# Four elementwise operations of a softplus go from VectorE to GpSimd in eight parts, in a software-pipelined scan stage

## The chip, the cores and the metric

The kernel runs on one core of a Trainium2 chip. The metric is device time in microseconds, the median of several executions; lower is better. The engines are named as the profile names them: PE is the matmul engine (PEld its weight loads), DVE is VectorE, ACT is ScalarE, POOL is GpSimd, and SP is the queue that issues most DMAs. Each engine works through its own instructions in the order in which they were written; semaphores tie the engines together.

## The reference

The program is two layers of a graph network with a mixture of experts behind each. Only the middle of the first layer matters here, a selective scan (Mamba) over 4096 tokens with 512 channels and 16 states per channel:

```python
u = silu(xconv)
dbc = u @ w_xp
dt = softplus(dbc[:, :DT_RANK] @ w_dt + b_dt)
dA = exp(dt[:, :, None] * A[None])
dBu = dt[:, :, None] * B[:, None, :] * u[:, :, None]
# scan over the tokens: h = dA*h + dBu ; y = h @ C
y = (ys + u * D_skip) * silu(z)
```

The change touches the softplus and the product dt·u. Everything else (the adjacency product before, the experts and the second layer behind) is the same program in both kernels.

## The kernel before, in words

**Tiling.** Tokens go through in 8 chunks of 512 (`CW`), numbered 0 to 7. The 512 channels are 4 blocks of 128 partitions, `m` = 0 to 3; blocks 0 and 1 are the first pair ("half 0"), 2 and 3 the second. Each chunk has 32 steps (`STEPS`); a step takes one channel block and two of the 16 states. Steps 0 to 15 of a chunk work on the first pair, steps 16 to 31 on the second.

**One step** (`Step`), for step n, is spread over four engines:

- POOL multiplies `du` (= dt·u, one block, used for both states) with the broadcast row of B into `db`, 128x1024 (L1354). The multiply of step n+1 is issued during step n. `db` has two buffers, so it must wait until step n-1 has read the same buffer.
- ACT makes the decays `da` = exp(dt·A), one 128x512 tile in PSUM per state (L1370), one step ahead, in three PSUM banks.
- DVE runs two scans in place over `db` (L1377), with `da` from PSUM, and then the product `hc` = `db`·`cb` (L1387). A small ACT copy saves the last column as state (L1383).
- POOL's queue issues a DMA that adds the second half of `hc` to the first (L1391, `pair`), one step late; PE then sums `hc` over the states with an identity matmul (L1404), up to three steps late.

B and C rows come in by broadcast DMAs on SP (L1350), double-buffered.

**The next chunk's front.** While chunk c is scanned, everything that chunk c+1 needs is made in between, at step numbers written out by hand in `Front.PLAN` and `Front.EARLY` (L899 to L914): "EARLY" pieces come between a step's scans and its product, the others after it. At step 26 ACT takes exp(-|x|) into `du`, at step 27 ("plus", L1071) `t1` = 1 + that, at step 28 ("log", L1075) the logarithm into `du`. Each is one 128x1024 instruction per pair of blocks. At steps 28 to 31 DVE runs `do_soft`, four operations, each once per pair, so eight 128x1024 instructions per chunk:

- soft 0 (L1081): `t1` = (`t1` - 1) - e, the rounding error of 1 + e with its sign turned, where e is the exponential,
- soft 1 (L1085): `du` = log - `t1`,
- soft 2 (L1087): `dt` = max(x, 0) + `du`, which is the softplus,
- soft 3 (L1089): `du` = `dt`·u.

At step 31 the EARLY piece comes ahead of the step's other work, since the multiply for the next chunk's step 0 needs `du` of the first pair. The second pair's `dt` and `du` are first used by work issued in step 15 of the next chunk. Chunk 0's front runs before the scan stage.

**Order.** In this stage PE, DVE, ACT and POOL keep the written order. In each step the loop at L1501 writes: the next step's inputs (L1524, B and C loads and the POOL multiply), the `pair` DMA of the step before (L1526), the scans with the next step's decays, the EARLY piece, the product, the gates of finished sums (L1413, a DVE multiply of a PSUM tile with `zs`), and the rest of the front. Adjacency matmuls for chunk c+2 (L871) fill PE.

**Buffers the change uses.** `t1` shares a slot (tag "tmp") with `xc`, which the next front takes at step 13. The pool tag "h" holds the normalised rows from step 9 until step 13 of a chunk.

Of the kernel before, what the change touches and what calls it, by code (L numbers as in the profile page):

```python
# [10 lines left out]
F32 = mybir.dt.float32  # L11
BF16 = mybir.dt.bfloat16
I32 = mybir.dt.int32
AF = mybir.ActivationFunctionType
ALU = mybir.AluOpType
# [4 lines left out]
P = 128  # L20
CW = 512
# [25 lines left out]
def kernel(ctx: ExitStack, tc: tile.TileContext, out: bass.AP, **a):  # L47
    nc = tc.nc
    x, adj, adjT = a["x"], a["adj"], a["adjT"]
# [28 lines left out]
    def load(pool, src, name, eng=None):  # L78
        t = pool.tile(list(src.shape), F32, name=name)
        (eng or nc.sync).dma_start(t, src)  # L80
        return t

    def load_bcast(pool, vec, name):
        t = pool.tile([P, vec.shape[1]], F32, name=name)
        nc.sync.dma_start(t, vec.to_broadcast([P, vec.shape[1]]))
        return t
# [696 lines left out]
    with ExitStack() as s1:  # L783
        wp = s1.enter_context(tc.tile_pool(name="w_gnn0", bufs=1))
        w1p = s1.enter_context(tc.tile_pool(name="work1", bufs=1))
# [53 lines left out]
        H = MB // 2  # L839
        GS = NS // 2  # L840
        STEPS = H * 2 * GS
# [9 lines left out]
        psts, fronts = {}, {}  # L851
# [41 lines left out]
        class Front:  # L893
# [175 lines left out]
            def do_plus(self):  # L1069
                for a in range(2):  # L1070
                    nc.scalar.activation(self.t1[:, a], self.du[a], AF.Identity, bias=1.0)  # L1071

            def do_log(self):
                for a in range(2):
                    nc.scalar.activation(self.du[a], self.du[a], AF.Ln, bias=1.0)  # L1075

            def do_soft(self, i):
                for a in range(2):
                    t1, dt, du = self.t1[:, a], self.dt[a], self.du[a]
                    if i == 0:  # L1080
                        nc.vector.scalar_tensor_tensor(  # L1081
                            t1, t1, -1.0, du, ALU.add, ALU.subtract
                        )
                    elif i == 1:
                        nc.vector.tensor_tensor(du, du, t1, ALU.subtract)  # L1085
                    elif i == 2:
                        nc.vector.tensor_tensor(dt, dt, du, ALU.add)  # L1087
                    else:
                        nc.vector.tensor_tensor(  # L1089
                            du, dt, self.us[:, a * H:a * H + H, :], ALU.mult  # L1090
                        )
                if i == 3:
                    fronts[self.c] = self

        def keep_gated(c):

            yd = dram.tile([P, MB, CW], F32, name=f"yd{c}")
            nc.sync.dma_start(yd, fronts[c].us)
            return yd
# [130 lines left out]


        SLOW = 3

        TAILS = {(NC - 2, i): 0 for i in (25, 26, 28)}
        TAILS.update({(NC - 2, i): 2 for i in range(29, STEPS)})
# [179 lines left out]
        with tc.manual_schedule(engines={  # L1415
# [13 lines left out]
            for _ in range(2 * NT + 2 - sum(FILLED.values())):  # L1429
                i = min(range(STEPS), key=lambda i: pe[i] - PE_RATIO * dve[i])  # L1430
# [4 lines left out]
            def advance(k=1, wait=False):  # L1435


                while k > 0:
                    k -= 1
                    if next(prop, None) and wait:  # L1440
                        break
                return k
# [19 lines left out]

            gate_w = load(const, a["L0_ffn_gate_w"], "gate_w")
            gate_b = load_bcast(const, a["L0_ffn_gate_b"], "gate_b")
            carry = wp.tile([P, MB, KC - 1], F32, name="carry")
            state = wp.tile([P, MB, NS], F32, name="state")

# [10 lines left out]
            fr = Front(0)  # L1478
# [22 lines left out]
            for n in range(NC * STEPS):  # L1501
                c, i = divmod(n, STEPS)
                if n == 0:
                    cur = Step(0, 0)
                    cur.inputs(None)
                    das = [cur.decay(0), cur.decay(1)]
                steps.append(cur)
                if i == 5 and c > 0:
                    if c < NC - 1:
                        kept[c - 1] = keep_gated(c - 1)  # L1510
                    else:
                        tails.extend(Tail(c - 1, hh) for hh in range(2))
                if i == 8 and c == NC - 2:
                    tails.extend(
                        Tail(k, hh, kept[k], k < SLOW) for k in range(c) for hh in range(2)
                    )
                if i == 8:
                    fr = Front(c + 1) if c + 1 < NC else None
                    prop = propagation(c + 2) if c + 2 < NC else iter(())
                if i == STEPS - 1 and fr is not None:  # L1520
                    fr.at(i, Front.EARLY)
                nxt = Step(*divmod(n + 1, STEPS)) if n + 1 < NC * STEPS else None
                if nxt is not None:
                    nxt.inputs(cur)  # L1524
                if n > 0:
                    steps[n - 1].pair()  # L1526
                old, das = das, []
                for j in range(2):
                    cur.scan(j, old[j])
                    if nxt is not None:  # L1530
                        das.append(nxt.decay(j))
                if 7 < i < STEPS - 1 and fr is not None:
                    fr.at(i, Front.EARLY)
                if c == NC - 1 and i in NORMS:
                    NORMS[i]()
                cur.product()
                for k in gated:
                    steps[k].gate()
                gated = []
                while summed < n - 1 and (summed < n - 3 or not steps[summed].paired):  # L1540
                    steps[summed].total()
                    gated.append(summed)
                    summed += 1
                if i < 8:
                    fronts[c].at(STEPS + i)
                elif fr is not None:
                    fr.at(i)
                for _ in range(TAILS.get((c, i), 1)):
                    Tail.step(tails)
                if c == NC - 1:  # L1550
                    for piece in NPIECES.get(i, ()):
                        piece()
                    if i == 22:
                        last = Last()
                        last.first(1)
                    elif i == 24:
                        last.fetch()
                    elif i == 25:
                        last.first(0)
                    elif i in (27, 28):  # L1560
                        last.residual(i - 27)
                owed = advance(pieces[i] + owed, True)
                if i == 7:
                    while owed:
                        owed = advance(owed, True)
                cur = nxt
            n = NC * STEPS
# [17 lines left out]
    wp = ctx.enter_context(tc.tile_pool(name="w_ffn0", bufs=1, reuse_waits="tile"))  # L1585
    early.close()
    with ExitStack() as s2:
# [309 lines left out]
        with tc.manual_schedule(engines={  # L1897
# [10 lines left out]
            for k, (c, j2) in enumerate(seq):  # L1908
# [11 lines left out]
                if k in ROUTES:  # L1920
                    b = ROUTES[k]
# [47 lines left out]
    with ExitStack() as s4:  # L1969
# [21 lines left out]
        ready, op = list(range(SPLIT)), []  # L1991
# [31 lines left out]
    with tc.If(again > 0):  # L2023
        with ExitStack() as s3:
# [3 lines left out]
            with tc.For_i(0, NT, 1) as i:  # L2028
                f = gp.tile([P, N], F32, name="f_all")
# [51 lines left out]
        with ExitStack() as s3:  # L2081
# [20 lines left out]
            op = s3.enter_context(tc.tile_pool(name="out2", bufs=1))  # L2102
# [71 lines left out]
```

## Time and profile before

| what | value |
|---|---|
| median of 6 runs | 2361.13 us (2353.97 to 2365.89) |
| the profiled execution | 2355.22 us |
| its span, first to last instruction | 2353.3 us |
| scan stage in the span | about 158 to 1244 us |
| one chunk in the steady part | 136.0 us (step 31's POOL multiply at 563.19, 699.20 and 835.21 us) |
| DVE, POOL, ACT, PE busy in 440 to 580 us (140 us) | 136.16, 107.52, 83.84, 135.52 us |
| TensorE clock granted in that stretch | 0.98 |

A timeline line gives the start in us from the span's start, the duration in us, the engine, the line of the kernel, the operation, the tiles and shapes, and in square brackets how long the engine was idle before it and what ended the wait. "x2" merges two neighbours of the same kind. A line of stretches gives, for PE, PEld, DVE, ACT and POOL, the busy time and the number of instructions, then the granted clock, the DMA share and GB/s. DVE instructions follow each other somewhat more closely than their durations say: an `hc` of 1.23 us is followed 1.14 us after its start.

### The profile page before, as it was taken

How to read it: one execution, taken by the hardware profiler on the slowest of the kernel's cores; microseconds unless marked ns; L12 is line 12 of the kernel's file. 1: busy time of each engine (PE TensorE's matmuls, PEld its weight loads, DVE VectorE, ACT ScalarE, POOL GpSimd, SP SyncE). 2: the span in 40 equal slices, each digit the busy share in tenths (PEclk: the TensorE clock that was granted, in tenths of full speed). 3: DMA queues.
4: the chain of work that ended last, by engine and by line, in shares of the span. 5: the costliest groups of instructions: out<-in, count | busy, mean ns of one | idle time of the engine just before them, and what ended most of it. 6: DMA issues, size and time to landing. Idle time of an engine off the chain costs nothing. (4 is left out here: it accounts for less than half of the span.)

```text
span 2353.3 us, 28092 instructions
## 1 busy us (share of the span) xinstructions
PE 2105.1 (89%) x8235; PEld 1498.8 (64%) x8235; DVE 1812.8 (77%) x3207; ACT 1193.4 (51%) x2064; POOL 1399.7 (59%) x1056
## 2 busy tenths in 40 slices
PE   7899999999999999997896899968869899799894
PEld 6665564656556565654564787855648678577773
DVE  6959999999999999999997887125228899854242
ACT  4145657565665755567672223214459578433221
POOL 1037778777777777786763444531357778745651
PEclk9999999999999999998897999988969999899997
DMA  8559999999999999998985999743345555476794
GB/s 285 172 156 258 234 271 242 272 245 250 271 238 272 244 273 244 250 268 237 280 260 168 312 335 321 232 157 109 128 123 176 165 165 171 122 229 213 232 317 153
DMA packets 302677, 532.29 MB, mean 226 GB/s; under 512 B 31323, under 2 KB 170575, under 8 KB 301616
## 3 DMA queue, kind: packets, MB, share of 16 engines
q1 hardware_dynamic: 244720, 416.84, 54.8%
q0 software_dynamic: 57792, 113.54, 21.8%
q8 instruction: 69, 1.13, 0.2%
q14 instruction: 96, 0.79, 0.1%
HBM read 434.34 MB, written 49.02 MB: 205 GB/s over the span
## 5 line engine op out<-in xcount | busy, mean ns | idle before, releaser
L1354 POOL TENSOR_TENSOR db<-du,bb 128x1024 f32<-128x1024 f32 x256 | 607.1, 2372 | 312.5 <-DVE hc L1387 75.6
L1377 DVE TENSOR_TENSOR_SCAN db<-da,state,db 128x512 f32<-128x512 f32 x512 | 627.4, 1267 | 20.2 <-ACT da L1370 18.0
L871 PE MATMUL pt<-at,gn 128*128 128x256 f32 x2048 | 481.6, 388 | 17.5 <-ACT gn L129 10.4
L871 PEld LDWEIGHTS pt<-at,gn 128*128 128x128 f32 x2048 | 398.7, 195 | 139.3 <-issue 62.7
L1370 ACT ACTIVATE da<-dt,negA 128x512 f32<-128x512 f32 x512 | 346.1, 688 | 245.7 <-DVE db L1377 235.9
L1387 DVE TENSOR_TENSOR hc<-db,cb 128x1024 f32<-128x1024 f32 x256 | 327.6, 1280 | 17.9 <-issue 0.4
L1864 PE MATMUL pf<-gn,f 128*128 128x256 f32 x1280 | 300.3, 393 | 27.5 <-issue 27.4
L1864 PEld LDWEIGHTS pf<-gn,f 128*128 128x128 f32 x1280 | 250.5, 197 | 71.9 <-issue 36.8
L1404 PE MATMUL psy<-hc,ident 128*128 128x512 f32 x560 | 291.6, 614 | 1.9 <-DMA hc<-hc 1.9
L712 PE MATMUL ps_h<-xkT,wk 128*128 128x256 f32 x864 | 215.5, 391 | 16.5 <-ACT hk L716 6.7
L697 PE MATMUL ps_y<-wk,hk 128*128 128x256 f32 x864 | 216.4, 385 | 3.9 <-issue 3.7
L702 DVE TENSOR_TENSOR yk<-ps_y,bk 128x512 f32<-128x512 f32 x73 | 50.4, 690 | 214.4 <-PE ps_y L697 146.9
L1391 POOL DMA_DIRECT2D hc<-hc x232 | 201.9, 870 | 0.2
L712 PEld LDWEIGHTS ps_h<-xkT,wk 128*128 128x128 f32 x864 | 159.2, 193 | 55.5 <-ACT hk L716 15.4
L1726 POOL DMA_INDIRECT x<-gnd,ls_idx x128 | 153.1, 1196 | 68.0 <-issue 22.6
L697 PEld LDWEIGHTS ps_y<-wk,hk 128*128 128x128 f32 x864 | 162.5, 193 | 27.1 <-issue 4.9
L1404 PEld LDWEIGHTS psy<-hc,ident 128*128 128x128 f32 x560 | 105.1, 194 | 82.4 <-issue 60.1
L1726 POOL DMA_INDIRECT ring<-gnd,ls_idx x88 | 110.5, 1255 | 53.5 <-DVE x L1742 31.7
L1846 ACT ACTIVATE f<-at 128x1024 f32<-128x1024 f32 x80 | 84.2, 1053 | 91.3 <-remote 51.1
L999 PE MATMUL ps_xz<-hT,w_in 128*128 128x512 f32 x256 | 117.0, 600 | 14.1 <-ACT hT L983 7.5
L716 ACT ACTIVATE hk<-ps_h,d0r_b 128x256 f32<-128x256 f32 x104 | 48.8, 472 | 136.2 <-PE ps_h L712 77.8
L1016 PE MATMUL ps_xz<-xc,dK 128*128 128x512 f32 x256 | 114.8, 592 | 0.0
(398 smaller groups left out, 2999.6 us busy)
## 6 DMA issues: line engine op xcount, KB each, us to landing
at<-in_adjT_dram SPq DMA_DIRECT2D x208, 512.0 KB
bb<-bcd SPq DMA_DIRECT2D x128, 512.0 KB
cb<-bcd SPq DMA_DIRECT2D x128, 512.0 KB
hc<-hc POOLq DMA_DIRECT2D x232, 256.0 KB
wk<-in_L_ffn_W_dram SPq DMA_DIRECT2D x70, 512.0 KB
wk<-in_L_ffn_expert_w_dram SPq DMA_DIRECT2D x114, 256.0 KB
ls_at<-in_adj_dram SPq DMA_DIRECT2D x32, 512.0 KB
hc<-in_adj_dram SPq DMA_DIRECT2D x16, 512.0 KB
```

Source lines behind the costliest of these rows:

```text
L697: nc.tensor.matmul(ps[:, j, :], hT[:, m, j * P:(j + 1) * P], w[:, m, :], start=(m == 0), stop=(m == kb_out - 1),)
L712: nc.tensor.matmul(ps[:, j, :], w[:, d, m * P:(m + 1) * P], xT[:, d, :], start=(d == 0), stop=(d == DB - 1),)
L871: nc.tensor.matmul(pt[:, k, :], xl[:, j, k * P:(k + 1) * P], at[:, jj, :], start=(j == 0 and k == 0), stop=(j == NT - 1 and k == DB - 1),)
L999: nc.tensor.matmul(ps, w_in[:, k, m * P:(m + 1) * P], self.hT[:, k, :], start=(k == 0), stop=(k == DB - 1),)
L1354: nc.gpsimd.tensor_tensor(self.db, self.f.du[self.half][:, self.mi:self.mi + 1, :].to_broadcast([P, 2, CW]), self.bb, ALU.mult,)
L1370: nc.scalar.activation(da, self.f.dt[self.half][:, self.mi, :], AF.Exp, scale=negA[:, self.m, n:n + 1])
L1377: nc.vector.tensor_tensor_scan(self.db[:, j, :], da, self.db[:, j, :], state[:, self.m, n:n + 1], ALU.mult, ALU.add,)
L1387: nc.vector.tensor_tensor(self.hc, self.db, self.cb, ALU.mult)
L1391: nc.gpsimd.dma_start(self.hc[:, 0, :], self.hc[:, 1, :], accum_op=ALU.add)
L1404: nc.tensor.matmul(f.psy[m], ident, self.hc[:, j, :], start=False, stop=(self.g == GS - 1 and j == last),)
L1726: nc.gpsimd.indirect_dma_start(out=to[:, :], out_offset=None, in_=gnd[:, :], in_offset=bass.IndirectOffsetOnAxis(ap=lists.idx[:, q, s:s + ...
L1864: nc.tensor.matmul(pf[:, t, :], f[:, jj, t * P:(t + 1) * P], gn[:, j, :], start=(j == 0 and t % 2 == 0), stop=(j == NT - 1 and t % 2 == 1),)
```

## The change

For chunks 1 to 7, DVE keeps `do_soft` for the first pair only. The second pair's four operations go to POOL, each cut into its two channel blocks: eight `tensor_tensor` instructions of 128x512. They are written into the loop right behind the `pair` DMA, so in POOL's order they come after the multiply for the next step and ahead of the one after it, in steps 29, 30 and 31 of the chunk in which the front is made and in steps 1, 2, 4, 6 and 8 of the next.

GpSimd gets plain two-input operations only. Soft 0 has three terms, so ACT subtracts 1 from the second pair's `t1` in an extra 128x1024 instruction at step 27 (with a constant tile `minus1` as its bias). The logarithm of the second pair is written to its own tile `ln1`, in the slot with tag "h", because e in `du` is still needed by a POOL operation that comes later. Chunk 0 is as before.

```diff
             def do_plus(self):
                 for a in range(2):
                     nc.scalar.activation(self.t1[:, a], self.du[a], AF.Identity, bias=1.0)
+                if self.c > 0:
+                    nc.scalar.activation(
+                        self.t1[:, 1], self.t1[:, 1], AF.Identity, bias=minus1[:, :1]
+                    )
 
             def do_log(self):
+                to = list(self.du)
+                if self.c > 0:
+                    to[1] = self.ln1 = w1p.tile([P, H, CW], F32, name="ln1", tag="h")
                 for a in range(2):
-                    nc.scalar.activation(self.du[a], self.du[a], AF.Ln, bias=1.0)
+                    nc.scalar.activation(to[a], self.du[a], AF.Ln, bias=1.0)
+
+            def spare(self, n):
+                i, b = divmod(n, H)
+                t1, dt, du = self.t1[:, 1, b, :], self.dt[1][:, b, :], self.du[1][:, b, :]
+                out, x, y, op = (
+                    (t1, t1, du, ALU.subtract), (du, self.ln1[:, b, :], t1, ALU.subtract),
+                    (dt, dt, du, ALU.add), (du, dt, self.us[:, H + b, :], ALU.mult),
+                )[i]
+                nc.gpsimd.tensor_tensor(out, x, y, op)
 
             def do_soft(self, i):
-                for a in range(2):
+                for a in range(2 if self.c == 0 else 1):
...
+        SPARES = {29: 0, 30: 1, 31: 2, 1: 3, 2: 4, 4: 5, 6: 6, 8: 7}
...
+            minus1 = wp.tile([P, 1], F32, name="minus1")
+            nc.gpsimd.memset(minus1, -1.0)
...
                 if n > 0:
                     steps[n - 1].pair()
+                if i in SPARES:
+                    f = fronts[c] if i < STEPS // 2 else fr
+                    if f is not None and f.c > 0:
+                        f.spare(SPARES[i])
```

The eight POOL parts are called spare 0 to spare 7 below, by the number that `SPARES` gives them.

## Prediction

> **What bounds the kernel now.** I read the page's busy shares first, then a table of stretches, the waits of DVE in the scan stage, and the timelines of DVE, POOL and ACT around a chunk's boundary.
>
> ```profile
> 440.00:580.00 140.00, 135.52 (x446) 83.83 (x445) 136.16 (x124) 83.84 (x147) 107.52 (x68) 0.98 0.97 257
> ...
> DVE db L1377 <- ACT da L1370: 18.0, 21, 2.4
> DVE db L1377 <- POOL db L1354: 2.2, 1, 2.2
> DVE hc L1387 <- issue: 0.4, 1, 0.4
> ```
>
> DVE is busy 136.16 of 140 us and in the whole stage (160 to 1240 us) waits 20.6 us on others, so an instruction taken off DVE looks worth its time. PE is busy 135.52 us: a gain above some 4.5 us per chunk would run into PE. POOL, at 107.52 us, looks free. A regular step shows that it isn't free in a useful place:
>
> ```profile
> 571.46 2.45 DVE L1377 TENSOR_TENSOR_SCAN db<-da,state,db 128x512 f32<-128x512 f32 x2
> 571.69 2.35 POOL L1354 TENSOR_TENSOR db<-du,bb 128x1024 f32<-128x1024 f32 x1 [0.52 <-issue]
> 573.99 0.87 POOL L1391 DMA_DIRECT2D hc<-hc  x1
> 574.00 1.22 DVE L1387 TENSOR_TENSOR hc<-db,cb 128x1024 f32<-128x1024 f32 x1
> 575.15 2.45 DVE L1377 TENSOR_TENSOR_SCAN db<-da,state,db 128x512 f32<-128x512 f32 x2
> 575.39 2.34 POOL L1354 TENSOR_TENSOR db<-du,bb 128x1024 f32<-128x1024 f32 x1 [0.53 <-DVE hc L1387]
> ```
>
> POOL's multiply starts 0.15 us after hc ends, runs exactly beside the two scans and ends (574.04) as the next hc starts (574.00). When the two meet, one of them is stretched:
>
> ```profile
> 613.32 1.93 POOL L961 TENSOR_TENSOR ln_rs<-ln_rs,mhalf 128x4 f32<-128x4 f32 x1 [2.66 <-DVE ln_rs L960]
> 615.24 2.34 POOL L1354 TENSOR_TENSOR db<-du,bb 128x1024 f32<-128x1024 f32 x1
> ...
> 616.82 1.84 DVE L1387 TENSOR_TENSOR hc<-db,cb 128x1024 f32<-128x1024 f32 x1
> ...
> 561.83 2.35 DVE L1089 TENSOR_TENSOR du<-dt,us 128x1024 f32<-128x1024 f32 x2
> 563.19 3.20 POOL L1354 TENSOR_TENSOR db<-du,bb 128x1024 f32<-128x1024 f32 x1 [3.81 <-issue]
> ```
>
> At 616.82 hc meets 0.76 us of a late multiply and takes 1.84 instead of 1.23, 0.61 longer. At 605.74 an overlap of 0.52 costs 0.37. At 563.19 POOL meets 0.99 us of DVE's soft 3 and takes 0.86 longer. So a DVE operation with two SBUF inputs (hc, the soft ones) and a POOL multiply take turns, the second losing the overlap less 0.13 us. Scans beside a multiply keep their 1.27 us; their `da` is in PSUM. I call what they take turns at "the port". In a regular step it is held 2.34 + 1.23 = 3.57 of 3.69 us: nearly as full as DVE.
>
> **The change, part by part.** Per chunk, for seven chunks, DVE loses four instructions of 1.21 to 1.22 us, 1.14 from start to start (two softs take 2.42, the next starts 2.34 after them): 4.56 us. The port loses 4 x 1.22 = 4.88 us and gains eight spares.
>
> *The spare's length s.* No 128x512 operation of POOL is in the trace. Half of the 128x1024 multiply is 1.17 us, the lower end (no fixed cost). The fixed cost lies between the smallest POOL instruction (MEMSET of 128x1, 0.098 us) and the longest memset mean (128x256, 0.363 us, part of it work): s is 1.27 to 1.53. I take 1.27, since the multiply's own start already contains its fixed cost, so half of it contains half.
>
> *Price c of one spare in a regular step.* It follows the pair DMA, which ends near 574.86, while hc holds the port to 575.22. It gets the port 0.13 before hc's end; the multiply follows at once (613.32 + 1.93 shows no gap); hc gets the port 0.13 before that ends. From hc's end to the next effective hc: s - 0.13 + 2.34 - 0.13 = s + 2.08; before it was 2.45 (571.55 to 574.00). So c = s - 0.37 = 0.90 us on DVE's path; doing the same half operation on DVE cost 0.57.
>
> *Steps 28 to 31.* Step 28 has no spare in front of it and loses 1.14. From the scans of step 29 to those of step 0 (17.64 us at 822.16 to 839.80) the port is the limit: three multiplies (7.02), six softs (7.3) and three hc (3.7) make 18.0, less the overlaps allowed. Three softs leave (3.66), spares 0 and 1 come (2.54): another 1.12 gained. Together -2.26.
>
> *Spares 2, 3, 4, 6* (felt in steps 0, 2, 3 and 7) meet regular steps: 4 x 0.90 = +3.60. *Spare 5* (felt in step 5) has a gate (L1413, 0.60 from start to start, one input in PSUM) ahead of the scans: 0.90 - 0.60 = +0.30.
>
> *Step 9's wait goes.* Its scans wait for ACT's decays:
>
> ```profile
> 869.22 0.19 ACT L1383 COPY state<-db 128x2 f32<-128x2 f32 x1 [0.54 <-DVE db L1377]
> 869.43 1.28 ACT L1023 ACT_TABLE_LOAD   x1
> ...
> 875.21 2.46 DVE L1377 TENSOR_TENSOR_SCAN db<-da,state,db 128x512 f32<-128x512 f32 x2 [1.08 <-ACT da L1370]
> 875.93 2.34 POOL L1354 TENSOR_TENSOR db<-du,bb 128x1024 f32<-128x1024 f32 x1 [2.15 <-ACT state L1383]
> ```
>
> That ACT run is tied to the scans of step 7 (8.53 us after their start at 866.68), which spare 6 doesn't move, while it moves hc of step 7. So 0.90 of the 1.08 is given back: -0.90. Spare 7 falls into POOL's 2.15 us of idle time there. Counted from the start of step 7's scans, hc of step 8 ended at 7.45 and now ends at 8.35; spare 7 ends at 8.35 - 0.13 + 1.27 = 9.49, and the multiply behind it started at 9.25: +0.24.
>
> Sum per chunk: -2.26 + 3.60 + 0.30 - 0.90 + 0.24 = +0.98; seven times +6.9. In the last chunk a 2.79 us power operation (POOL, 1122.93) stands between spare 3 and the multiply: spare 3 would end at 1123.44 + 1.27 = 1124.71, so everything behind moves 1.78 instead of 0.90: +0.9. Total +7.8 us.
>
> *Costed at nothing.* ACT's extra 128x1024 (1.06 us, 0.98 after overlap): it moves the decays of step 30 from 825.42 to 826.40, where DVE would be ready at 825.72; the port holds soft 2 to about 829 anyway. If the port did not, it would cost 0.68. The second pair's results are due in step 15, spare 7 is over in step 9. The slots of `t1` and `ln1` are free after spare 3, long before steps 9 and 13 ask for them. Pair DMAs go out up to 0.90 later against a DVE that is as late; PE sums three steps behind (11 us) and waited 1.9 us for them in all. On SP, the B load for steps 4 and 5 leaves at 570.39 and is used at 579.06; 0.9 us of 8.7 is slack. The memset of `minus1` (0.1 us) is ahead of the stage.
>
> *A rule against the change.* The Trainium skill ("Perfetto Trace Analysis", Optimizing Scalar/DVE Operations) warns that the two engines share an SBUF read port, so moving work between them may not help; "SBUF — State Buffer" (Who interferes with whom) says that the second to come is blocked until the first has finished. By that full block, without the measured 0.13, c would be 1.16 and the sum 7 x 2.5 + 1 = +19 us; the rows above decide for the 0.13.
>
> The profiled execution took 2355.22 us, 5.9 below the median of 2361.13. The sum makes it 2363.0, and the median 2369.
>
> **Rivals.** *A, the spares hide (faster).* Place: POOL's 0.5 us of idle time per step and the time beside the scans. If subtract, add and multiply on 128x512 did not hold up hc, DVE would keep 4.56 less the 0.68 at step 30, 3.88 per chunk: -27 us, 2334, just inside PE's 4.5. For it: DVE is the busiest engine and waits for POOL once. Against it: every hc that meets a multiply by 0.2 us or more is stretched. It decides below c = 0.78 (the sum is -4.66 + 6c with s = c + 0.37), that is s = 1.15.
>
> *B, dearer spares.* With s = 1.53, c is 1.16: -1.14 - 0.60 + 4.64 + 0.56 - 1.08 + 0.76 = +3.1 per chunk, +23 us, 2384. For it: a small POOL instruction has a cost that the trace doesn't show. Against it: the multiply after the power operation starts without a gap.
>
> *C, a wash.* With s = 1.17, c is 0.80: -1.14 - 1.32 + 3.20 + 0.20 - 0.80 + 0.04 = +0.2 per chunk, +2 us, 2363.
>
> **How the numbers follow.** Forecast with its own band of +4 to +14 (2365 to 2375): 0.50; C, -7 to +4: 0.16; A: 0.16; B, above +14: 0.18. About 0.3% (7 us) is what a measurement tells from no change. Slower by more: B and 0.32 of the forecast, 0.50. Within: C and 0.18 of the forecast, 0.34. Faster: 0.16. The range 2346 to 2386 reaches past B's price and into A, of which it leaves out the larger part (0.12), and 0.06 above.
>
> **What the profile after would show.** The four soft groups with 9 instead of 16 instructions; 56 POOL `tensor_tensor` of 128x512 at about 1.27 us, longer where they begin inside an hc; hc's mean up from 1280 ns by some 100 (about five times 0.9 in 32, seven chunks), several per chunk near 2.1 us; the ACT wait in step 9 nearly gone; chunks of about 137.0 us instead of 136.0, with steps 28 to 31 shorter by 2.3 and steps 0 to 9 longer by 3.2. I am wrong if hc keeps 1.23 us behind a spare (A), or if spares take over 1.5 us (B), or if DVE begins to wait for ACT in step 30 or for POOL ahead of its scans.

## The result and the profile after

The changed kernel takes 2375.6 us (median of 20 executions, 2368.69 to 2387.85) against 2359.68 us before (median of 46): a ratio of 1.0067, 95% interval 1.0051 to 1.0082, so about 15.9 us slower. That is inside the range and on the forecast's side, but twice the predicted +7.8 us, and just above the band of +4 to +14 us that the prediction gave to its own forecast. The profiled execution took 2382.29 us, 6.7 above its median; that of before was 5.9 under the median known then, so the two profiles differ by more (27 us) than the kernels do. I compare stages and steps instead of spans.

The group of `hc` on the page, after (busy time, mean ns of one, and idle time before it):

```profile
L1405 DVE TENSOR_TENSOR hc<-db,cb 128x1024 f32<-128x1024 f32 x256 | 376.9, 1472 | 17.8 <-issue 0.4
```

`hc` (L1405, which was L1387) went from a mean of 1280 ns to 1472 ns: 256 of them make 49 us that no new work asked for. The table of stretches, after, for the whole scan stage, from the start of the first `hc` to the start of the last:

```profile
160.30:1269.30 1109.00, 1032.91 (x3421) 639.72 (x3420) 1069.38 (x933) 683.36 (x1288) 888.47 (x553) 0.96 0.93 248
```

The same stage, before:

```profile
161.50:1248.10 1086.60, 1025.55 (x3421) 637.69 (x3420) 1049.34 (x962) 674.10 (x1281) 814.91 (x497) 0.97 0.93 254
```

The stage grew from 1086.6 to 1109.0 us. DVE has 28 instructions less in it (29 by where the stretch is cut) and is busy 20 us longer: what it no longer computes, it more than pays back in longer `hc`. Of the 22 us, 4.4 arise in chunk 0 up to its step 27, which the change doesn't touch; the other profiled executions with the full adjacency product show between -0.1 and +3.4 there, so the profile of before was among the quickest in that chunk. A difference between two stages holds this scatter, and I give the chunk 0 share beside it below. The waits of DVE, after, in the scan stage:

```profile
DVE db L1395 <- ACT da L1388: 19.3, 19, 5.4
```

They were 18.0 us before: the loss is not a new wait. It sits inside the durations of `hc`. The timeline around a regular meeting (steps 31 and 0) and around step 4, after:

```profile
572.75 1.23 DVE L1405 TENSOR_TENSOR hc<-db,cb 128x1024 f32<-128x1024 f32 x1
573.32 1.78 POOL L1092 TENSOR_TENSOR du<-ln,t 128x512 f32<-128x512 f32 x1
...
575.06 2.35 POOL L1372 TENSOR_TENSOR db<-du,bb 128x1024 f32<-128x1024 f32 x1
...
576.44 2.06 DVE L1405 TENSOR_TENSOR hc<-db,cb 128x1024 f32<-128x1024 f32 x1
...
593.67 0.87 POOL L1409 DMA_DIRECT2D hc<-hc  x1
594.22 2.72 DVE L1405 TENSOR_TENSOR hc<-db,cb 128x1024 f32<-128x1024 f32 x1
594.26 1.58 POOL L1092 TENSOR_TENSOR dt<-dt,du 128x512 f32<-128x512 f32 x1
```

The upper half is the price c. The spare starts inside an `hc`, waits for it (1.78 in the record; `hc` ends at 573.98, less 0.13, so 1.25 of its own until 575.10), the multiply follows at once, and the next `hc`, at 576.44, takes 2.06 instead of 1.23: 0.83 lost. The lower half is spare 5. Here `hc` starts at 594.22, the spare 0.04 us later, and it is `hc` that waits: 594.26 + 1.58 - 0.13 + 1.23 = 596.94, which is where its 2.72 end. It loses 1.49.

To see where a chunk's time goes I took the start of every `hc` from both timelines and subtracted, counting from step 27. From there through step 13 of chunk 3, in us against before:

| part | predicted | measured (after) |
|---|---|---|
| steps 28 to 31 | -2.26 | -1.99 |
| spares 2, 3, 4, 6 in regular steps | 4 x 0.90 = +3.60 | 0.83 + 0.82 + 0.85 + 0.84 = +3.34 |
| spare 5 (at step 4, felt in step 5) | +0.30 | +1.48 |
| given back at step 9's wait | -0.90 | -0.82 |
| spare 7 | +0.24 | +0.12 |
| sum of a chunk | +0.98 | +2.13 |

The seven chunks show 2.13, 2.72, 2.14, 2.81, 3.93, 2.15 and 2.52 in this profile (18.4 in all), and 2.13, 2.47, 2.15, 2.12, 2.61, 2.15 and 2.50 in a second one of the same kernel (below), which add up to 16.1. Chunks 2, 4 and 5 of this profile are longer mainly because DVE waits more for its decays at step 9 (0.96, 0.87 and 2.55 us, against 0.26 in chunk 3); the last has a power operation on POOL. The medians differ by 15.9 us in the first comparison and by 20.1 in the second.

### The profile page after: what moved, and what is told of

Same layout as the page of the kernel before. It is cut to its first block, busy times and chain, and to the rows that moved or that the text cites. A ratio compares the mean times of both kernels' runs of the same rounds, so it can differ in the third digit from the quotient of the medians.

```text
span 2380.3 us, 28134 instructions
## 1 busy us (share of the span) xinstructions
PE 2108.3 (89%) x8235; PEld 1499.1 (63%) x8235; DVE 1832.9 (77%) x3179; ACT 1203.2 (51%) x2071; POOL 1475.1 (62%) x1113
## 3 DMA queue, kind: packets, MB, share of 16 engines
q8 instruction: 69, 1.13, 0.2%
## 5 line engine op out<-in xcount | busy, mean ns | idle before, releaser
L1405 DVE TENSOR_TENSOR hc<-db,cb 128x1024 f32<-128x1024 f32 x256 | 376.9, 1472 | 17.8 <-issue 0.4
```

Source lines behind the costliest of these rows:

```text
L1405: nc.vector.tensor_tensor(self.hc, self.db, self.cb, ALU.mult)
```

## The experiments

Every run shares its chip with executions of the kernel before, and each ratio is to those. Where a kernel computes something else that sends tokens to other experts later, its total is no measure and I read the scan stage alone.

### The changed kernel without its spares

```diff
                     if f is not None and f.c > 0:
-                        f.spare(SPARES[i])
+                        pass
```

> The changed kernel without its eight GpSimd parts; the second pair's softplus of chunks 1 to 7 is left unfinished (dt and du keep what ACT wrote). It prices what DVE alone gains. Theory (turns between POOL's multiplies and DVE's two-input operations): DVE loses 4 x 1.14 = 4.56 us per chunk, ACT's extra instruction holds the scans of step 30 back by up to 0.7, so -3.9 per chunk, -27 us in seven; PE (135.5 busy of 140 us) may keep some of that, so -20 to -27. The changed kernel's +16 us would then be +36 to +43 us of POOL parts minus this gain. Rival 1 (ACT's extra instruction and the ln1 tile are what costs): no better than before, 0 to +10 us. Rival 2 (PE is the bound): a gain under 10 us.

The total (2348.42 us, ratio 1.0182, 1.0165 to 1.0199) can't be read, since the second pair's softplus stays unfinished and what follows differs. The stage is 1083.7 us against 1086.6 before: with four DVE instructions less in each chunk and nothing in their place it gains 3 us, not the 27 of rival A. Chunk 0 is 3.2 us longer here, so the seven chunks that differ gain 6.1 us, and the last alone gains 4.4 of them. By `hc` starts, chunks 1 to 6 are 3.07 us ahead up to step 7 and stand at -0.42, -0.67, +0.48, -1.01, +0.34 and -0.38 by step 13; the last, which has no adjacency work, is at -3.63 there. The waits in 300 to 1250 us, without the spares:

```profile
DVE db L1395 <- ACT da L1388: 33.5, 25, 3.6
...
ACT zs L1012 <- PE ps_xz L999: 17.8, 12, 2.6
```

Before, the same two lines were 15.1 and 1.7 us. The timeline of steps 8 and 9, without the spares:

```profile
594.21 0.58 ACT L1012 COPY zs<-ps_xz 128x512 f32<-128x512 f32 x1 [2.60 <-PE ps_xz L999]
...
596.40 1.31 ACT L1388 ACTIVATE da<-dt,negA 128x512 f32<-128x512 f32 x2
...
597.20 2.46 DVE L1395 TENSOR_TENSOR_SCAN db<-da,state,db 128x512 f32<-128x512 f32 x2 [0.88 <-ACT da L1388]
...
604.65 2.46 DVE L1395 TENSOR_TENSOR_SCAN db<-da,state,db 128x512 f32<-128x512 f32 x2 [3.31 <-ACT da L1388]
```

ACT's copies of `ps_xz` wait for a late PE, the decays stand behind them in ACT's order, and DVE's scans wait for the decays. So DVE and "the port" stop being the bound after about 3 us of a chunk; by these waits PE is next.

### A quarter of the adjacency matmuls left out of four kernels

The stall above is put down to PE. To test that, I made PE's load lighter in the kernel before, the changed kernel, the changed kernel without spares, and a variant with spare 5 in step 3 (its own section is below).

```diff
-                    for jj in range(4):
+                    for jj in range(3):
...
-                                start=(j == 0 and k == 0), stop=(j == NT - 1 and k == DB - 1),
+                                start=(j == 0 and k == 0), stop=(j == NT - 2 and k == DB - 1),
```

> The kernel before with every fourth matmul of the adjacency product left out (the product is then incomplete, the loads are not), the reference point for the next three. It takes about 25% of the adjacency work of TensorE out of the scan stage. Theory P (what eats gains at steps 8 and 9 is a late TensorE, through the copy of ps_xz on ScalarE and the decays): before lost next to nothing to it in its profiled run, so its scan stage (first to last hc, 1086.6 us) becomes 1082 to 1086, its step-9 wait for the decays (1.08) stays, since that one is ScalarE's table load and not TensorE. Rival Q (VectorE and GpSimd themselves, or ScalarE alone): the same.

> The changed kernel with the same quarter of the adjacency matmuls left out. Theory P: every chunk ends 2.1 later than in before_light, without the 2.7 to 3.9 of single chunks: the stage is 7 x 2.13 + 0.4 = 15 us longer. Rival Q: the single long chunks stay, 19 us or more.

> The changed kernel without the eight parts (the second pair's softplus stays unfinished), with the same quarter of the adjacency matmuls left out. Theory P: the 3.07 us a chunk that it held up to step 8 are kept through steps 8 and 9: the stage is 7 x 3.07 + 0.5 = 22 us shorter than before_light (at least 15), and the time at TensorE in the waits nearly goes. Rival Q: it loses them in steps 8 and 9 as with the full product and the stage is within 5 us of before_light.

> The variant with spare 5 in step 3, with the same quarter of the adjacency matmuls left out. Theory P: every chunk ends 0.95 later than in before_light, also the two that ended 2.7 and 3.9 later with the full product: the stage is 7 to 7.5 us longer, which is the prediction's sum of 0.98 a chunk. Rival Q: chunks of +2.7 and +3.9 stay, the stage is 11 us or more longer.

Each of the four ran once, so only their profiles are read. Stages, from the first `hc` to the last: before 1087.8 us, changed 1103.7 (+15.8), spare 5 in step 3 1093.6 (+5.8), no spares 1074.0 (-13.8). Before itself came out at 1087.8, a little above the expected 1082 to 1086. The changed kernel and the spare 5 variant land within 2 us of the sums 15 and 7 to 7.5. Chunk by chunk the agreement is looser: up to step 13 the seven chunks add up to 17.9 and 9.1, and 3 to 4 us are given back at later steps. One long chunk stays in each of them (+3.4 and +2.2), where theory P had none: in it the `hc` of step 8 starts 0.44 us late, spare 7 follows 0.24 us behind it, and that `hc` takes 2.9. Without the spares the gain grew from 3 to 13.8 us (in the seven chunks that differ from 6.1 to 15.1), so some 9 us of what the stall ate came back with a lighter PE; but 22, or at least 15, was expected. The rest goes at another place. The timeline of ACT and DVE, without spares and with the lighter product:

```profile
592.45 0.59 ACT L877 COPY pts<-pt 128x512 f32<-128x512 f32 x1 [4.54 <-PE pt L871]
...
593.74 2.46 DVE L1395 TENSOR_TENSOR_SCAN db<-da,state,db 128x512 f32<-128x512 f32 x2 [1.09 <-ACT da L1388]
```

ACT waits 4.54 us for the last adjacency matmul and holds the decays of step 2. PE is busy 960 of 1074 us in this stage, at a granted clock of 0.92, and the DMA engines 0.94 of the time. That ACT and DVE wait for the adjacency product next is shown; whether its matmuls or its loads come last in it is not settled.

### Extra multiplies, the softplus left on DVE

Eight POOL multiplies of 128x512 at the same places into a tile that nobody reads, the kernel before otherwise.

```diff
+                if self.c > 0:
+                    self.extra = w1p.tile([P, H, CW], F32, name="extra", tag="h")
...
+            def spare(self, n):
+                b = n % H
+                u = self.us[:, H + b, :]
+                nc.gpsimd.tensor_tensor(self.extra[:, b, :], u, u, ALU.mult)
...
+        SPARES = {29: 0, 30: 1, 31: 2, 1: 3, 2: 4, 4: 5, 6: 6, 8: 7}
...
+                if i in SPARES:
+                    f = fronts[c] if i < STEPS // 2 else fr
+                    if f is not None and f.c > 0:
+                        f.spare(SPARES[i])
```

> The kernel before with eight extra 128x512 two-input multiplies on POOL at the places of the spares, into a tile that nobody reads; DVE keeps all its soft operations and ACT gets nothing. Theory: per chunk spares 2, 3, 4 and 6 cost 0.83 each, spare 5 meets hc of step 4 head on (1.49 in the changed kernel's trace), 0.83 is given back in step 9, spare 7 costs 0.13, and spares 0 and 1 go into steps where the port is full with six softs, about 1.2 each: 3.32 + 1.49 - 0.83 + 0.13 + 2.4 = +6.5 per chunk, +46 us. Rival (POOL has 0.5 us to spare per step and the cost comes from elsewhere): under +10 us.

2352.5 us, ratio 1.0203 (1.0183 to 1.0223): 47 us by the ratio, 44.5 by the medians, for 56 instructions that nothing waits for, 0.8 us each. Six of the seven chunks lose 5.6 to 6.0 us up to step 13, where 6.5 was expected. The timeline at steps 31 and 4, extra multiplies:

```profile
723.97 2.74 DVE L1395 TENSOR_TENSOR hc<-db,cb 128x1024 f32<-128x1024 f32 x1
724.25 1.36 POOL L1082 TENSOR_TENSOR extra<-us 128x512 f32<-128x512 f32 x1
...
745.27 0.87 POOL L1399 DMA_DIRECT2D hc<-hc  x1
745.83 2.48 DVE L1395 TENSOR_TENSOR hc<-db,cb 128x1024 f32<-128x1024 f32 x1
745.87 1.35 POOL L1082 TENSOR_TENSOR extra<-us 128x512 f32<-128x512 f32 x1
```

At step 4 the pattern of spare 5 repeats: 0.04 us after the start of `hc`, and `hc` loses 1.25 us. At step 31 the extra multiply starts 0.28 us after `hc`, and it is again `hc` that waits: 724.25 + 1.36 - 0.13 + 1.23 = 726.71, where its 2.74 end. So nearly equal starts are not the condition. Over the runs here with such parts, a part of 128x512 that stands right behind a pair DMA and starts 0.04 to 0.45 us after `hc` makes `hc` wait (39 meetings, none the other way), and one that starts 0.56 us after it or later lets it go first (205 meetings, none the other way). A multiply that starts from an idle POOL does not do this: at 563.19, before, it starts 0.23 us after a soft 3 (562.96) and waits for it. In a regular step without a gate the loss is 0.60, less than c because this multiply, whose two inputs are one tensor, is shorter (about 1.0 us).

### Extra memsets

The same with a memset of 128x1024 (1.26 us, as long as a spare, but it reads nothing).

```diff
+            def spare(self, n):
+                nc.gpsimd.memset(self.extra, 0.0)
```

> The kernel before with eight extra POOL memsets of 128x1024 at the places of the spares (about 1.0 to 1.3 us each by the 0.20 us of 128x128 and 0.31 to 0.36 us of 128x256): the same delay of POOL's queue, but an instruction that reads nothing. Theory 1 (turns are taken for reading only): a memset runs beside hc, so the multiply behind it starts only some 0.4 us late and hc loses about 0.34; in steps 29 and 30 it fits into 2.7 us of idle POOL time; spare 5's place costs nothing: 4 x 0.34 - 0.34 = +1.0 per chunk, +7 us, and no hc is stretched while a memset alone runs. Theory 2 (any POOL instruction takes turns with a two-input DVE operation): like the two-input multiplies, +40 us or more, hc stretched to 2.0 and 2.7 us at the same places. Theory 3 (only the queue's order counts, no turns): about 0, hc stays 1.23.

2317.18 us, ratio 1.0042 (1.0026 to 1.0058): 9.7 us by the ratio, 9.2 by the medians, near the 7 of theory 1. The timeline at step 4, extra memsets:

```profile
728.10 1.23 DVE L1393 TENSOR_TENSOR hc<-db,cb 128x1024 f32<-128x1024 f32 x1
728.11 1.26 POOL L1080 MEMSET extra<- 128x1024 f32 x1
```

Side by side for the whole of `hc`, and `hc` keeps its 1.23 us where beside the multiply it took 2.48. What the memsets cost is POOL's time: the multiply behind one starts later and meets the next `hc` (1.54 to 1.66 in three places of a chunk, given back in part at step 9). So `hc` takes turns with an instruction that reads, and not with one that only writes. The Trainium skill ("SBUF — State Buffer", Who interferes with whom) says that a DVE instruction with two SBUF inputs contends with a GpSimd instruction that reads SBUF and not with one that only writes it; 2.48 against 1.23 agree. It also says that issue order decides who blocks; by the record's starts (594.22 and 594.26, 723.97 and 724.25) the POOL operation would have waited, and here it was `hc`.

### ACT's extra instruction alone

```diff
+                if self.c > 0:
+                    nc.scalar.activation(self.t1[:, 1], self.t1[:, 1], AF.Identity)
```

> The kernel before with one more 128x1024 ACT instruction at step 27 (t1 of the second pair copied onto itself), chunks 1 to 7: the ACT part of the change alone. Theory: the decays of step 30 are ready at 825.4 in the trace of before and wanted at 828.0, so 0.98 more costs nothing: 0 us (-2 to +2). Rival (ACT is near its limit there): up to 0.98 x 7 = +7 us.

2310.56 us, ratio 1.0009 (0.9997 to 1.0022); from step 27 to step 13 five of the seven chunks move by 0.03 us at most, the last two by +0.18 and -0.10. ACT's part of the change costs nothing in this place, as the prediction had it.

### Spare 5 moved to step 3

```diff
-        SPARES = {29: 0, 30: 1, 31: 2, 1: 3, 2: 4, 4: 5, 6: 6, 8: 7}
+        SPARES = {29: 0, 30: 1, 31: 2, 1: 3, 2: 4, 3: 5, 6: 6, 8: 7}
```

> The changed kernel with spare 5 written into step 3 instead of step 4. In the changed kernel's trace spare 5 started at 594.26, 0.04 us after hc of step 4 began, and hc took 2.72 us (1.49 more), because the gate ahead of that step's scans lets POOL finish its multiply and its DMA issue early. Theory (who comes first takes the port): in step 3 the spare comes 0.6 us behind hc, waits for its end, and the gate's 0.60 us then hides most of it: 0.83 - 0.60 = 0.23 instead of 1.49, so -1.26 per chunk and -9 us against the changed kernel: about +7 us against before (ratio 1.003), no hc of 2.7 us left. Rival (a spare costs the same wherever it stands): unchanged, +16 us, ratio 1.0067.

The first comparison gave 2377.14 us, ratio 1.0071 (1.0044 to 1.0098), where about 1.003 was expected: a miss on the time. Its stage was 1100.7 us, 8.3 below the changed kernel's 1109.0, where 9 was expected; but 2.3 of the 8.3 lie in chunk 0, which is the same in both. Because of that contradiction I ran it and the changed kernel again on one chip.

> The changed kernel once more, unaltered, so that it and the variant with spare 5 in step 3 share one chip. Ratio 1.0067 as before (1.005 to 1.008), scan stage 1105 to 1110 us.

> The variant with spare 5 in step 3 once more. Theory S (what its first comparison hid is the scatter between executions and chips): its stage is 8 us shorter than that of the changed kernel run beside it, and its median 5 to 10 us lower, a ratio to before of about 1.003. Rival T (the stalls behind TensorE at steps 8 and 9 eat the saving in most executions): the stage of one profiled execution may be shorter, the median is within 3 us of the changed kernel's.

The changed kernel: 2395.03 us, ratio 1.0083 (1.0053 to 1.0113), stage 1105.1. The variant: 2396.0 us, ratio 1.0081 (1.0059 to 1.0103), stage 1097.0. The timeline of POOL and DVE at steps 3 and 4 with spare 5 moved (second run):

```profile
586.09 1.67 POOL L1092 TENSOR_TENSOR dt<-dt,du 128x512 f32<-128x512 f32 x1
...
589.62 1.52 DVE L1405 TENSOR_TENSOR hc<-db,cb 128x1024 f32<-128x1024 f32 x1
...
594.14 1.23 DVE L1405 TENSOR_TENSOR hc<-db,cb 128x1024 f32<-128x1024 f32 x1
```

The `hc` that took 2.72 takes 1.52. The shift is +0.79 at step 5 instead of +2.0 in each of the seven chunks of both runs, and five of seven chunks in either run end between 0.92 and 1.31, around the prediction's 0.98. The other two end at 2.67 and 3.95 in the first run and at 2.70 and 2.70 in the second: there the saving is lost again at steps 8 and 9. In one of the two (chunk 5, then chunk 1) DVE waits 3.66 and 2.19 us for its decays at step 9, behind ACT's waits for `ps_xz` and for the adjacency product (0.91 and 0.90 us for the latter). In the other (chunk 4 both times) the `hc` of step 8 waits 0.48 and 0.35 us for its C rows, so that spare 7 starts 0.21 and 0.34 us behind it, and it takes 2.87 and 3.01. The stages differ by 8.3, 8.1 and (with the lighter product, above) 10 us; without chunk 0, where both do the same work, by 6.0, 4.6 and 9.6, of the 8.4 that 1.2 us in each of seven chunks would make. So the saving at step 4 is shown in every chunk, and part of it is lost again in the stage with the full product. In the total nothing of it is seen. The two stretches where the second pair of profiles differs, first the changed kernel's (the stage, and 300 us beginning 300 us behind it):

```profile
161.90:1267.00 1105.10, 1029.92 (x3421) 638.52 (x3420) 1068.87 (x934) 682.66 (x1288) 888.50 (x553) 0.96 0.93 249
...
1567.00:1867.00 300.00, 232.34 (x938) 178.24 (x936) 151.80 (x393) 153.47 (x193) 128.76 (x125) 0.86 0.43 134
```

and the variant's:

```profile
161.30:1258.30 1097.00, 1027.46 (x3421) 637.15 (x3420) 1062.11 (x933) 682.66 (x1287) 888.10 (x553) 0.96 0.93 251
...
1558.30:1858.30 300.00, 224.51 (x876) 168.53 (x875) 142.37 (x374) 139.94 (x180) 126.62 (x126) 0.84 0.41 126
```

Behind the stage, in code that is the same, the changed kernel took 1117.5 us and the variant 1133.1, with 938 and 876 matmuls done in 300 us and a granted clock of 0.86 and 0.84. In the first pair of profiles (from two chips) it was the other way round, 1111.0 and 1105.0. So that part scatters by more than 8 us between executions. Theory S is half right (the stage is 8.1 us shorter, 3.5 of them in chunk 0, and the median no lower). Rival T had the right median, and its stalls are there, but they stand out in two chunks of seven and don't eat the whole saving. With 7 and 12 executions the scatter of the medians should be smaller than 8 us, and both comparisons say the same; whether a shorter scan stage is paid for by a lower clock behind it, or chance did it twice, stays open. What I can claim is 4.6 to 6 us of the stage with the full product, not of the total.

### Fewer parts, placed where `hc` doesn't meet them

The kernel before, with only soft 2 and soft 3 of the second pair on POOL, as four parts: one in step 3 (ahead of a gate), one in step 8 and two in step 10, where POOL is idle. No extra ACT instruction and no extra tile is needed.

```diff
+            def spare(self, n):
+                i, b = divmod(n, H)
+                dt, du = self.dt[1][:, b, :], self.du[1][:, b, :]
+                if i == 0:
+                    nc.gpsimd.tensor_tensor(dt, dt, du, ALU.add)
+                else:
+                    nc.gpsimd.tensor_tensor(du, dt, self.us[:, H + b, :], ALU.mult)
...
-                for a in range(2):
+                for a in range(2 if self.c == 0 or i < 2 else 1):
...
+        SPARES = {3: (0,), 8: (1,), 10: (2, 3)}
...
+                for part in SPARES.get(i, ()):
+                    if c > 0:
+                        fronts[c].spare(part)
```

> The kernel before with only the second pair's last two operations (dt and du) on POOL, as four 128x512 parts in places where DVE has work that doesn't need the port: one in step 3 (ahead of the gate), one in step 8 (POOL waits 1.9 us for ACT), two in step 10 (DVE has 2.3 us of statistics ahead of hc). Softs 0 and 1 stay on DVE, ACT gets nothing. Theory: DVE loses 2 x 1.14 = 2.28 us per chunk, the parts cost 0.23 + 0 + 0: -2.05 per chunk, -14 us, ratio 0.994. Rival (moving this work to POOL costs wherever it is put): four parts at 0.83 less 2.28, +1.0 per chunk, +7 us, ratio 1.003.

2357.12 us, ratio 0.9977 (0.9959 to 0.9995), 4.6 us (by the medians) under its kernel before: faster than the kernel before by a third of the 14 us expected, and so than the changed kernel, which was slower than before in both of its comparisons. The timeline, four parts:

```profile
714.60 1.52 DVE L1396 TENSOR_TENSOR hc<-db,cb 128x1024 f32<-128x1024 f32 x1
...
730.77 1.75 POOL L1081 TENSOR_TENSOR dt<-dt,du 128x512 f32<-128x512 f32 x1
732.48 2.46 DVE L1386 TENSOR_TENSOR_SCAN db<-da,state,db 128x512 f32<-128x512 f32 x2 [1.08 <-ACT da L1379]
...
739.67 2.80 POOL L1083 TENSOR_TENSOR du<-dt,us 128x512 f32<-128x512 f32 x2
...
998.87 1.58 POOL L1081 TENSOR_TENSOR dt<-dt,du 128x512 f32<-128x512 f32 x1
999.21 2.33 DVE L1396 TENSOR_TENSOR hc<-db,cb 128x1024 f32<-128x1024 f32 x1 [1.03 <-DMA cb<-bcd]
```

The part in step 3 costs 0.29 (1.52 for 1.23). The one in step 8 ends while DVE waits 1.08 us for its decays, and the two in step 10 run beside DVE's statistics instructions: both cost nothing. Chunks 1 to 5 gain 1.9 to 2.0 us each (2.28 off in steps 30 and 31, 0.29 paid). Chunk 6 gains 1.1: the `hc` of step 8 (999.21) waits 1.03 us for its C rows, so that the part is ahead of it, and then takes 2.33. The last chunk, 2.4 ahead at step 0, is 0.8 behind at step 13, by a wait in step 4 and longer `hc` in steps 4, 10 and 11 (it has no statistics in step 10), but is 1.2 ahead again at step 15 and 1.8 at step 27. The stage is 1076.9 us, 9.7 shorter than before; as chunk 0 is 2.9 longer here, the seven chunks that differ gain 12.6, close to the 14 of the working. Behind it this profiled execution took 1125.0 us instead of 1105.2, so here too the total shows less than the stage, and why is not settled.

## Why the prediction was right, and where its size was off

- **The mechanism** was right: POOL's work isn't free, DVE operations with two SBUF inputs and POOL multiplies take turns. The extra multiplies cost 47 us with DVE's list unchanged and the memsets 9.7, so it is the turns and not POOL's load that cost most. Rival A as worked out (-27 us) is refuted by the changed kernel: `hc` takes 2.06 behind a spare.
- **The spare's length** of 1.27 was right (1.25), and so B (1.53) and C (1.17) are out as mechanisms. The prediction's sign of B, spares over 1.5 us, did come: the record gives all 56 between 1.56 and 1.80. But that holds the wait for `hc` or a soft operation, and 0.3 us in which the record still shows the pair DMA; of two parts that follow each other in step 10 of the four-part variant, the second ends 1.22 after the first (2.80 less 1.58). The price c was 0.83 to 0.85 instead of 0.90, and so not the 1.16 of a full block, although the total is nearer to the +19 us of that than to +7.8. The total, +15.9, lies just above the forecast's own band and so in the part that the prediction gave to B, for a reason that isn't B's: the direction was right by the mechanism, the size was not.
- **The term that was mis-sized** is the spare 5 one, "0.90 - 0.60 = +0.30". It measured +1.48, and 7 x 1.18 = 8.3 us is as much as the gap between 7.8 and the 16.1 of the second profile; what else differs there (0.8 more in two long chunks, 0.5 less in the last chunk's extra, small terms) happens to cancel. The step that failed is the order of the two. In the profile of before, step 4 reads:

```profile
585.04 0.88 POOL L1391 DMA_DIRECT2D hc<-hc  x1
...
585.60 1.23 DVE L1387 TENSOR_TENSOR hc<-db,cb 128x1024 f32<-128x1024 f32 x1
```

The working let a spare come when the DMA's record ends; here that is 585.92, 0.32 after `hc` has begun, so the spare would find the port taken and wait, and the gate's 0.60 would hide most of its price. In the record POOL's next instruction starts already 0.59 to 0.60 after the start of the DMA (593.67 to 594.26; 745.27 to 745.87 with the extra multiplies), and `hc` 0.55 after it, and it was `hc` that waited, as it did in every meeting up to 0.45 us apart. What decides the turn inside that time the runs don't show. The prediction took one order as certain instead of pricing both. Moved one step ahead, the same spare costs 0.29.

- **Steps 28 to 31** gave -1.99 instead of -2.26. The prediction priced ACT's extra instruction at nothing and named 0.68 as the cost if the port didn't hold DVE. Without the spares, step 30 shows it: three operations give 1.13 each, the fourth is lost to a wait of 0.91 for decays that stand behind ACT's longer chain and to soft 2, which then meets a late multiply (1.77 instead of 1.21), 4.56 - 3.07 = 1.49 in all. With the spares that wait isn't there (the scans of step 30 start at 562.89 without idle time, the decays end at 562.70), so the 0.27 missing are not ACT's; spares 0 and 1 each make an `hc` take 2.29 there, and the sum had priced that a little too low.
- **The wait at step 9** went from 0.88 to 0.26 in chunk 3, and with 0.20 of an `hc` that no longer meets a late multiply, -0.82 was given back (-0.90 predicted). **Spare 7** cost 0.12 (0.24).
- **The profile's signs**: 9 instead of 16 instructions in the soft groups, several `hc` near 2.06, and chunks longer by 2.1 instead of 1.0. Of the mean of `hc`, 192 ns were added where 100 were expected; besides the mis-sized 2.72 these are the two `hc` of 2.29 in steps 29 and 30, where spares 0 and 1 get between a soft operation and `hc`; the sum had these in steps 28 to 31, and the sign had left them out.
- **Rival A's price** also failed: "just inside PE's 4.5" us per chunk took PE's idle time as one block. It isn't; with the waits for `ps_xz` and `pt` at steps 8 and 9, chunks 1 to 6 keep 0.3 us on average of the 3.07 that DVE gained.

## What to carry to other kernels

An engine's idle share says nothing of its idle places: look at which operation stands beside each gap, and move work only to gaps beside operations that don't take turns with it (scans reading PSUM, waits for a third engine). When two operations that exclude each other would start within half a microsecond, price both orders; here one cost 0.3 and the other 1.5 us, and the one whose record began first was the loser at up to 0.45 us. And before pricing an engine's relief, ask which engine is next in line at each wait and what stands ahead of it in ACT's order, since 3.07 us won per chunk came to 0.3 in six chunks of seven.

## What the runs showed of the hardware that I had not expected

- The record of POOL's next instruction starts 0.57 to 0.64 us after the start of a DMA issue that the record mostly gives 0.85 to 0.91 us. Whether POOL works for it from then on isn't shown: spare 5, which had the port, takes 1.58 from there and 1.30 from the end of the DMA's record.
- The later one in the record can have the port: with starts of 594.22 (DVE) and 594.26 (POOL) `hc` took 2.72, and with 723.97 and 724.25 it took 2.74.
- A POOL memset as long as a spare, running beside a whole `hc`, leaves it at 1.23 us.
- A POOL multiply of a tensor with itself takes about 1.0 us, one of two tensors 1.25.
- Behind the scan stage the same code took 1105 to 1133 us in the profiled executions on chips where the kernel before takes 2360 to 2375 us, with the granted clock in one 300 us stretch at 0.84 to 0.87: more scatter than the effect measured here.
